# Column and row scans on one core: the order of layer 1's last stages, and how x is brought in

## Chip, cores and metric

The kernel runs on one core of a Trainium2 chip. The metric is the device time of one execution in microseconds, as the median of the runs.

## What is computed

Two layers of the same form. Each normalises x (32 images, 48 channels, 64 rows, 128 columns) over 16 channel groups, runs four scans over the result, and adds the outcome to x. The step of a scan is a convolution with five taps over the other axis, on all 48 channels, plus a bias and the next line of input:

```
def step(w, b):
    def f(carry, inp):
        nxt = inp + _conv1d(carry, w, b)
        return (nxt, nxt)
...
x = x + _L0_conv_ref(_gn(x), ...)      # down, up, right, left
x = x + _L1_conv_ref(_gn(x), ...)
```

Down and up run over the 64 rows (126 steps), right and left over the 128 columns (254 steps). Every step needs the one before it.

## The kernel before

The batch is cut into four groups of eight images. A **row stage** runs down and up for one group, a **column stage** right and left for a pair of groups at once. `PHASES` lists twelve stages, and they run one after the other; I call them r00, r01, c00 and so on: r or c, the layer, then the group or the pair. The profile's tiles carry the same names (`step_00d` is a down step of group 0 in layer 0, with `u`, `r`, `l` for the other ways).

A step (`step`, L824) is nine fp32 products on TensorE into three PSUM tiles; for each tile VectorE then adds bias and input in one operation (L846) and writes the next line. That chain of 2024 steps sets the order of everything else. Around it a list of dated entries, the agenda, holds all other work: `at(t, fn, ...)` puts an entry at step t, and `catch_up` emits the entries that are due before each step. `in_order` keeps each engine's instructions in that order, so what an engine does first is written by hand, and a DMA that waits holds up the later DMAs of its queue. Most DMAs go on SP's queue, some on ScalarE's (ACT), and the loads of a seam partly on POOL's.

**On chip** three slots of 48 KB a partition hold lines. A row stage uses two; a column stage cuts the width into four quarters, keeps three in slots and sends the first to DRAM and back (`spill_unit`). A quarter has six units: three blocks of 128 partitions in each of two groups.

**A row stage** (`plan_rows`, L949) loads its rows 16 at a time from DRAM (`move_rows`, 20 DMAs on SP), normalises them on ScalarE (`scale_rows`, L667) and writes the result of the up scan back. **A column stage** (`plan_cols`, L992) loads quarters, and in the left scan takes each unit through: a residual comes in (`load_residual`), POOL adds it (`add_residual`, L769), and the sum is kept. In layer 0 it goes to DRAM as layer 1's input (`keep_result`), and statistics of it are taken on VectorE (even units) and ScalarE (odd ones). In layer 1 the unit is permuted to the order of the output on POOL and ScalarE (`permute_unit`, L794) and stored (`store_result`), in pieces of 128 bytes. For the first pair, c10, three of the four quarters are instead held in DRAM (`HELD`, `hold_result`, one DMA a unit on ACT's queue) and passed on to the output during c11 (`let_result`, on SP's queue).

Where a column stage follows the row stage of its own second group (`follows`), the last rows go straight from SBUF to the columns' slot (`send_row`, `send_rest`): I call this a **seam**. c00 and c01 have one. c11 follows c10, and c10 follows r13; neither has one.

**The start** (`first_group`, L1126) brings in group 0: sixteen DMAs of 768 KB load one image each, first the upper 16 rows of both halves of the height for all eight images, then the other 16 (I call each of these loads an image). VectorE takes statistics of each as it lands. Rows are then brought to the order of the scan: POOL and ScalarE copy a row's pieces (`permute`, L621), `put_out` stores the row in DRAM, and `move_rows` loads it back with channels and columns spread over partitions. Rows 0 to 3 go through TensorE instead (`rows_by_product`, L1210, with the result copied by ScalarE). The weights of the first scan are laid out by TensorE too (`place_kernel`). At the end stands `scaling` (L341), which averages the statistics on TensorE and turns them into a scale and an offset.

x in DRAM is kept by channel and half of the height, 96 partitions at a time:

```
source = [
    [
        dram.tile([PX, MOIETY], F32, tag=f"xin{g}", name=f"xin{g}")[:, 0 : CHANNEL // 2]
        for g in range(NGRP)
    ],
    kept("mid"),
]
```

Of the kernel before, what the change touches and what calls it, by code (L numbers as in the profile page):

```python
# [78 lines left out]
def weight_runs():  # L79
# [33 lines left out]
    ("rows", 1, 2),  # L113
    ("rows", 1, 3),
    ("cols", 1, 0),
# [5 lines left out]
def kernel(  # L121
# [65 lines left out]
    def kept(name):  # L187
# [6 lines left out]
    MOIETY = (CHANNEL + PAD) // 2  # L194
    source = [
        [
            dram.tile([PX, MOIETY], F32, tag=f"xin{g}", name=f"xin{g}")[:, 0 : CHANNEL // 2]
            for g in range(NGRP)
        ],
        kept("mid"),  # L200
    ]
# [11 lines left out]
    HELD = (2, 1, 0)  # L213
# [13 lines left out]
    def x_by_row(t, e, h0, h1):  # L227

        s, h = divmod(h0, HALF)
        t = t.rearrange("(c s) (i q a e n) -> s e a c i q n", s=2, i=E8, q=NQ, a=NH // 2, e=E8)  # L230
        t = t[s, e, h // E8, :, h % E8 : h % E8 + h1 - h0]
        return t.rearrange("c i q n -> c (i q) n")

    def x_by_col(t, e, j):


        return t.rearrange("(c s) (i q n) -> i q c s n", s=2, i=E8, q=NQ)[e, j]

    def lines(t, h0, h1):

        t = t.rearrange("p (i q a n) -> a p i q n", i=E8, q=NQ, a=NH // 2)[h0 // E8]
        return t[:, h0 % E8 : h0 % E8 + h1 - h0].rearrange("p i q n -> p (i q) n")
# [70 lines left out]
    def load_masks(dma):  # L313
        for s in range(2):
            dma(sided(mask_sb)[s], mask[SIDES[s], SIDES[0]])

# [24 lines left out]
    def scaling(key, layer, g, averages, masks, slack=0):  # L341
# [5 lines left out]
        pool = nc.gpsimd  # L347
# [19 lines left out]
        def small(name):  # L367
# [5 lines left out]
        scale, offset = (  # L373
            stat_pool.tile(
                [FULL, NG, GB], F32, tag=f"{t}{layer}{g}", name=f"{t}{layer}{g}"
            )
            for t in ("scale", "offset")
        )
        coeffs[layer, g] = scale, offset
        mean, var = ps[:, 1 : 1 + NG], ps[:, 2 + NG :]  # L380
        spare = small("dev")
        dev = spare[0 : FULL if n > 1 else PX, 0:n]
        if not slack:
            far = ps[0:PX, 1 + NG : 2 + NG]
            nc.vector.tensor_tensor(far, mean_p, ps[0:PX, 0:1], ALU.subtract)
            nc.vector.tensor_tensor(dev, mean_p, ps[0:PX, 0:1], ALU.subtract)
            nc.vector.tensor_tensor(far, far, dev, ALU.mult)
            nc.vector.tensor_tensor(dev, far, var_p, ALU.add)
            yield
            expand(var, dev[:, 0])  # L390
            yield
            nc.vector.tensor_scalar(var, var, GN_EPS, None, ALU.add)
            r0 = small("std")
            nc.scalar.activation(r0, var, AF.Sqrt)
            expand(mean, mean_p[:, 0])
            yield
            yield
            nc.vector.reciprocal(r0, r0)
            nc.vector.tensor_tensor(var, var, r0, ALU.mult)
            nc.vector.tensor_tensor(var, var, r0, ALU.mult)  # L400
            nc.vector.tensor_scalar(var, var, -0.5, 1.5, ALU.mult, ALU.add)
            nc.vector.tensor_tensor(scale, var, r0, ALU.mult)
            nc.vector.tensor_tensor(offset, mean, scale, ALU.mult)
            nc.vector.tensor_scalar(offset, offset, -1.0, None, ALU.mult)
            return
        mean_s = small("mean")
        if n > 1:
            mean_c = stat_tile([PX, GB], "mean_c", key)
            nc.vector.tensor_copy(mean_c, ps[0:PX, 0])
            yield  # L410
            expand(mean, mean_c)
            yield
            nc.vector.tensor_tensor(dev, mean_p, mean, ALU.subtract)
            nc.vector.tensor_copy(mean_s, mean)
        else:
            nc.vector.tensor_tensor(dev, mean_p, ps[0:PX, 0:1], ALU.subtract)
        pool.tensor_tensor(dev, dev, dev, ALU.mult)
# [5 lines left out]
        if n == 1:  # L423
            expand(var, dev[:, 0])
        else:
# [5 lines left out]
            expand(var, var_c)  # L431
        yield
        var_s = small("var")
        nc.vector.tensor_scalar(var_s, var, GN_EPS, None, ALU.add)
        std = small("std")
        nc.scalar.activation(std, var_s, AF.Sqrt)
        if n == 1:
            expand(mean, mean_p[:, 0])
        yield
        if n == 1:  # L440
            nc.vector.tensor_copy(mean_s, mean)
# [6 lines left out]
        pool.tensor_tensor(t0, var_s, r0, ALU.mult)  # L448
        pool.tensor_tensor(t0, t0, r0, ALU.mult)
        yield  # L450
        pool.tensor_scalar(t0, t0, -0.5, 1.5, ALU.mult, ALU.add)
        pool.tensor_tensor(scale, r0, t0, ALU.mult)
        pool.tensor_tensor(offset, mean_s, scale, ALU.mult)
        pool.tensor_scalar(offset, offset, -1.0, None, ALU.mult)

# [167 lines left out]
    def put_out(g, r, perm):  # L623


        n = perm.shape[-1] // (W * GB)
        dma(lines(source[0][g], r, r + n), perm.rearrange("p (m n) -> p m n", n=LINE))
# [8 lines left out]
    def move_rows(k, h0, h1, to_dram, q=None):  # L636
# [4 lines left out]
        for h in range(h0, h1, E8):  # L641
            end = min(h1, h + E8)
            for o in range(NG):
                for e, c0, c1, p0 in pieces(o):
                    here = view[p0 : p0 + c1 - c0, o, h % HALF : h % HALF + end - h]
                    if to_dram or layer:
                        there = by_row(t, e, h, end, q)[c0:c1]
                    else:
                        there = x_by_row(t, e, h, end)[c0:c1]
# [29 lines left out]

    def scale_first(k, h1, split):  # L680

# [310 lines left out]
    def plan_cols(k, t0, prev):  # L992
# [39 lines left out]
        if layer:  # L1032
            tiles += spare_tiles[0 : 2 if final else 1]
# [303 lines left out]
```

## Time and profile before

| | us |
|---|---|
| median of 3 runs (4236.17, 4236.53, 4246.85) | 4236.53 |
| the profiled execution | 4246.85 |
| its span, first to last instruction | 4245.1 |

What lies around the span is 1.75 us. The stages of that execution, from the first to the last sum that VectorE makes in each:

| stage | from | to | length |
|---|---|---|---|
| start | 0 | 74.09 | 74.09 |
| r00 | 74.09 | 351.10 | 277.01 |
| r01 | 352.01 | 600.05 | 248.04 |
| c00 | 608.37 | 1123.23 | 514.86 |
| r02 | 1124.08 | 1391.78 | 267.70 |
| r10 | 1392.57 | 1643.85 | 251.28 |
| r03 | 1644.64 | 1892.73 | 248.09 |
| c01 | 1900.02 | 2403.76 | 503.74 |
| r11 | 2404.62 | 2667.45 | 262.83 |
| r12 | 2668.24 | 2916.30 | 248.06 |
| r13 | 2917.09 | 3165.15 | 248.06 |
| c10 | 3165.86 | 3661.80 | 495.94 |
| c11 | 3662.66 | 4166.24 | 503.58 |
| tail | 4166.24 | 4245.10 | 78.86 |

How to read it: the shortest row and column stages are those in which no step waited, so the length of another one less that is what its steps waited for, together with the slower steps that follow a wait. In lines of the timeline the columns are start, duration, engine, line, operation, tiles and count; brackets give the idle time before and what ended it. In lines by stage they are the window, its length, then busy time and count of PE, PEld, DVE, ACT and POOL, the granted clock, the share of the 16 DMA engines that was busy, and GB/s.

### The profile page before, as it was taken

Reading aid. Unit: us, or ns where it says so; the run is one execution under the profiler, and the core shown is the slowest. Engines: PE = TensorE matmul, PEld = TensorE weight load, DVE = VectorE, ACT = ScalarE, POOL = GpSimd, SP = SyncE. Lnnn points to the kernel's source line nnn. Section 1 sums busy time; section 2 is a strip of 40 time slices with the busy share of each in tenths; the row PEclk is TensorE's granted clock in tenths of the full one; section 3 lists DMA queues with packets and bytes.
Section 4 is the critical chain, followed back from the end, with each engine's and each line's share of the span. In section 5 each row is a group of like instructions: output and inputs, shape, how many; then the busy total and the mean of one; then the engine's idle time right before and its main releaser. Section 6 shows DMA issues by size and latency. Waiting matters only on the chain. (4 is left out here: it accounts for less than half of the span.)

```text
span 4245.1 us, 90421 instructions
## 1 busy us (share of the span) xinstructions
PE 4072.4 (96%) x36704; PEld 4050.5 (95%) x36704; DVE 2142.6 (50%) x6517; ACT 1346.5 (32%) x2680; POOL 870.8 (21%) x879
## 2 busy tenths in 40 slices
PE   6999999899999999999999999999999999999992
PEld 5899999899999999999999999999999999999992
DVE  6454444457654454444447654444444444444443
ACT  4675001436885446000007863603000012110122
POOL 5460011334423020010014410000000024510352
PEclk9999999999999999999999999999999999999996
DMA  9999668868979999358409979839288049999999
GB/s 229 187 212 155 109 121 178 228 151 261 199 166 181 165 166 152 64 100 182 120 12 274 207 147 155 131 63 162 41 146 188 1 84 251 244 251 159 173 209 182
DMA packets 2129378, 679.80 MB, mean 160 GB/s; under 512 B 2012497, under 2 KB 2062913, under 8 KB 2095169
## 3 DMA queue, kind: packets, MB, share of 16 engines
q1 hardware_dynamic: 2026720, 582.07, 70.7%
q10 hardware_dynamic: 99680, 86.43, 9.5%
q8 instruction: 289, 4.73, 0.5%
q0 software_dynamic: 2560, 5.51, 0.5%
q14 instruction: 129, 1.05, 0.1%
HBM read 397.00 MB, written 295.14 MB: 163 GB/s over the span
## 5 line engine op out<-in xcount | busy, mean ns | idle before, releaser
L667 ACT ACTIVATE arena<-arena,offset,scale 128x256 f32<-128x256 f32 (+2 forms) x816 | 576.6, 800 | 355.0 <-DVE arena L846 122.1
L769 POOL TENSOR_TENSOR arena<-arena 128x2048 f32<-128x2048 f32 x80 | 363.0, 4553 | 1400.7 <-PE step_10l L837 437.5
L621 POOL COPY arena<-arena 96x256 f32<-96x256 f32 x452 | 267.5, 646 | 519.8 <-DMA arena<-in_x 481.0
L564 ACT ACTIVATE early<-arena 128x256 f32<-128x256 f32 x192 | 129.5, 675 | 450.6 <-POOL arena L769 444.5
L837 PE MATMUL step_00r<-arena,early 128*128 128x128 f32 x2286 | 253.6, 275 | 18.9 <-DVE arena L846 11.2
L837 PEld LDWEIGHTS step_00r<-arena,early 128*128 128x128 f32 x2286 | 252.9, 186 | 19.6 <-DVE arena L846 13.3
L837 PE MATMUL step_01r<-arena,early 128*128 128x128 f32 x2286 | 253.2, 274 | 9.6 <-DMA arena<-arena 5.8
L837 PEld LDWEIGHTS step_01r<-arena,early 128*128 128x128 f32 x2286 | 252.4, 186 | 10.3 <-issue 5.3
L837 PE MATMUL step_11r<-arena,early 128*128 128x128 f32 x2286 | 251.1, 273 | 5.2 <-DVE arena L846 5.2
L837 PEld LDWEIGHTS step_11r<-arena,early 128*128 128x128 f32 x2286 | 250.6, 185 | 5.6 <-DVE arena L846 5.6
L837 PE MATMUL step_00l<-arena,wleft 128*128 128x128 f32 x2286 | 249.1, 272 | 0.0
L837 PEld LDWEIGHTS step_00l<-arena,wleft 128*128 128x128 f32 x2286 | 248.6, 184 | 0.0
L837 PE MATMUL step_10l<-arena,wleft 128*128 128x128 f32 x2286 | 248.5, 272 | 0.0
L837 PE MATMUL step_10r<-arena,early 128*128 128x128 f32 x2286 | 248.5, 272 | 0.0
L837 PE MATMUL step_11l<-arena,wleft 128*128 128x128 f32 x2286 | 248.5, 272 | 0.0
L837 PE MATMUL step_01l<-arena,wleft 128*128 128x128 f32 x2286 | 248.4, 272 | 0.0
L837 PEld LDWEIGHTS step_10l<-arena,wleft 128*128 128x128 f32 x2286 | 248.4, 184 | 0.0
L837 PEld LDWEIGHTS step_10r<-arena,early 128*128 128x128 f32 x2286 | 248.4, 184 | 0.0
L837 PEld LDWEIGHTS step_11l<-arena,wleft 128*128 128x128 f32 x2286 | 248.4, 184 | 0.0
L837 PEld LDWEIGHTS step_01l<-arena,wleft 128*128 128x128 f32 x2286 | 248.4, 184 | 0.0
L794 ACT COPY arena<-arena 128x256 f32<-128x256 f32 x172 | 99.4, 655 | 400.9 <-POOL arena L769 136.9
L261 ACT COPY early<-arena 128x1 f32<-128x1 f32 x2 | 0.4, 192 | 657.3 <-DVE arena L846 657.3
(203 smaller groups left out, 7163.7 us busy)
## 6 DMA issues: line engine op xcount, KB each, us to landing
arena<-in_x SPq DMA_DIRECT2D x24, 1536.0 KB, 11.6
xin<-arena SPq DMA_DIRECT2D x48, 768.0 KB, 5.4
arena<-xin SPq DMA_DIRECT2D x96, 384.0 KB, 8.2
mid<-arena SPq DMA_DIRECT2D x96, 384.0 KB, 7.7
arena<-mid SPq DMA_DIRECT2D x192, 192.0 KB, 4.3
upb<-arena SPq DMA_DIRECT2D x192, 192.0 KB, 3.9
arena<-upb SPq DMA_DIRECT2D x96, 384.0 KB, 12.1
arena<-xin SPq DMA_DIRECT2D x186, 192.0 KB, 4.3
```

Source lines behind the costliest of these rows:

```text
L261: fn(*args)
L564: nc.scalar.activation(junk[:, 0:n], view[:, b], AF.Identity, accum_out=self.sum[:, i, j : j + 1])
L621: copy(dst[:, r, q], src[:, r0 + r, q])
L667: nc.scalar.activation(args[0], args[0], AF.Identity, bias=args[2], scale=args[1])
L769: eng.tensor_tensor(unit, unit, nat, ALU.add)
L794: copy(by_w(perm)[:, a], src[:, a])
L837: nc.tensor.matmul(part(whole(ps[o])[0:m], -s), weights[:, i, at : at + m], part(src(i), s), start=seen[o] == 1, stop=seen[o] == left[o],)
```

## The change

In layer 1 the rows of the fourth group (r13) move between the columns of the two pairs: r12, c10, r13, c11. So c11 gets a seam. All four quarters of c10 are held in DRAM; its residuals and the held units go on SP's queue, with four buffers instead of five. They are passed to the output on ACT's queue: the first 30 of 64 items during r13 from step 48, the others during c11 from step 36 to 122. Ahead of each stands a one-element copy on ScalarE that reads the result of a given step (`pace`), so that the item is not issued before that step.

x in DRAM is kept by channel alone, so `put_out` makes two DMAs of 48 partitions where it made one of 96, and the loads of rows and residuals lose their own forms. At the start the first weights come by small DMAs on ACT's queue (taps to DRAM, then 25 pieces to SBUF) instead of through TensorE, the masks and ten bias pieces behind them; rows 4 to 7 come by a second product on TensorE instead of through DRAM; rows 0 to 7 of the first eight loads are copied through DRAM at the very end, for the rows 32 to 39 that they hold besides (before, rows 0 to 3 at the end and 4 to 7 early); and the scale is applied to the first four rows by VectorE alone, row 0 first. `scaling` has one form for all groups. The early activation that loaded ScalarE's table for square roots is gone.

```diff
     ("rows", 1, 2),
+    ("cols", 1, 0),
     ("rows", 1, 3),
-    ("cols", 1, 0),
     ("cols", 1, 1),
...
-    HELD = (2, 1, 0)
+    HELD = (3, 2, 1, 0)
...
     def hold_result(j, i, perm):
         o, half = UNITS[i]
-        dma(held[j, half][o], perm, nc.scalar)
+        dma(held[j, half][o], perm)
...
-                dma(in_output(j, half, e)[c0 * NH : c1 * NH], src[at : at + (c1 - c0) * NH])
+                dst = in_output(j, half, e)[c0 * NH : c1 * NH]
+                dma(dst, src[at : at + (c1 - c0) * NH], nc.scalar)
+
+    def pace(k, n):
+
+        if PHASES[k][0] == "rows":
+            done = row(k, n + 1 if n < H - 1 else 2 * H - 3 - n)[:, 0, 0:1]
+        else:
+            kb, e = divmod(n + 1, E8)
+            j, kk = divmod(kb, KQ)
+            done = quarter(k, j)[:, 0, 0, e * RUN + kk * GB :][:, 0:1]
+        nc.scalar.copy(junk[:, BN - 1 :], done)
...
-        if layer:
-            tiles += spare_tiles[0 : 2 if final else 1]
+        if final:
+            tiles += spare_tiles
...
-                at(end + 63 + 1.9 * n, let_result, *what)
+                if n < 30:
+                    m = 48 + int(2.3 * n)
+                    at(end + m, pace, k + 1, m - 2)
+                    at(end + m, let_result, *what)
+                else:
+                    m = 36 + int(2.6 * (n - 30))
+                    at(end + 2 * (H - 1) + m, pace, k + 2, m - 2)
+                    at(end + 2 * (H - 1) + m, let_result, *what)
...
-            if layer:
-                dma(here, by_col(t, e, j)[c0:c1], nc.scalar)
-            else:
-                dma(here.rearrange("p (s n) -> p s n", s=2), x_by_col(t, e, j)[c0:c1])
+            dma(nat[p0 : p0 + c1 - c0], by_col(t, e, j)[c0:c1], nc.scalar if k == len(PHASES) - 1 else None)
...
+    source = [kept("xin"), kept("mid")]
...
-        dma(lines(source[0][g], r, r + n), perm.rearrange("p (m n) -> p m n", n=LINE))
+        for s in range(2):
+            h = s * HALF + r
+            dma(
+                lines(source[0][g], h, h + n),
+                sided(perm)[s].rearrange("p (m n) -> p m n", n=LINE),
+            )
...
-        pool, act = nc.gpsimd, nc.scalar
-        load_kernel()
         for i in range(2):
             for b in range(GB):
...
+                take_in(0, i * rows, parts[i], slice(b, b + 1))
+        nc.vector.memset(spare["right"], 0.0)
+        nc.vector.memset(spare["left"], 0.0)
+        load_weights("down0", 0, DOWN, aside)
+        load_constants(aside)
         make_ident()
-        place_kernel()
-        spread_masks()
         for b in range(GB):
             stats.take(0, parts[0], b)
-        put_rows(0, 4, 8, free, pool, act)
+        permute_rows(0, 8, 12, free, nc.gpsimd, nc.scalar)
+        put_rows(0, 8, 12, free)
         rows_by_product(0, 4)
-        put_rows(0, 8, 14, free, pool, act)
-        put_rows(0, 14, 16, free, pool)
-        move_rows(0, 4, 8, False)
-        move_rows(0, 8, 16, False)
+        spread_masks()
+        permute_rows(0, 12, 15, free, nc.gpsimd, nc.scalar)
+        put_rows(0, 12, 15, free)
+        permute_rows(0, 15, 16, free, nc.gpsimd)
+        put_rows(0, 15, 16, free)
+        rows_by_product(4, 4)
...
+        move_rows(0, 8, 16, False)
+        for r in range(0, 8, 2):
+            permute_rows(1, r, r + 2, free, nc.gpsimd)
+            put_rows(1, r, r + 2, free)
         for _ in scaling("x0", 0, 0, stats, x_masks):
             pass
-        scale_first(0, 4, 5)
+        scale_at_once(0, 0, 1, nc.vector)
+        scale_at_once(0, 1, 4, nc.vector)
         scale_rows(0, 4, 8)
         scale_rows(0, 8, 16)
-        put_rows(1, 0, 8, free, pool)
         move_rows(0, 16, 24, False)
         scale_rows(0, 16, 24)
...
-        put_rows(0, 0, 4, later, pool)
-        move_rows(0, 32, 40, False)
+        permute_rows(0, 0, 4, later, nc.gpsimd)
+        put_rows(0, 0, 4, later)
+        permute_rows(0, 4, 8, later, nc.gpsimd)
+        put_rows(0, 4, 8, later)
+        move_rows(0, 32, 48, False)
         scale_rows(0, 32, 40)
```

## Prediction

> **What bounds the kernel now.** I read the page first, then the busy time by stage, then the timeline of each engine over the first 75 us and over the starts of the stages.
>
> ```profile
> PE 4072.4 (96%) x36704; PEld 4050.5 (95%) x36704; DVE 2142.6 (50%) x6517; ACT 1346.5 (32%) x2680; POOL 870.8 (21%) x879
> ```
>
> ```profile
> core 0: us, PE busy (x) PEld busy (x) DVE busy (x) ACT busy (x) POOL busy (x), PEclk, DMA share, GB/s
> 0.00:74.09 74.09, 45.26 (x122) 30.02 (x123) 52.55 (x104) 20.97 (x43) 26.71 (x66) 1.00 0.96 246
> 74.09:351.10 277.01, 259.73 (x2277) 257.42 (x2277) 125.75 (x399) 189.37 (x431) 145.33 (x204) 0.97 0.97 194
> 1124.08:1391.78 267.70, 261.10 (x2324) 260.13 (x2323) 139.44 (x443) 185.49 (x367) 79.28 (x106) 0.97 0.91 177
> 1900.02:2403.76 503.74, 499.14 (x4567) 498.76 (x4567) 281.79 (x833) 130.28 (x307) 82.03 (x19) 0.99 0.63 153
> 2404.62:2667.45 262.83, 257.47 (x2324) 256.69 (x2323) 138.92 (x443) 154.64 (x261) 33.32 (x27) 0.99 0.95 159
> 2917.09:3165.15 248.06, 248.06 (x2264) 248.06 (x2263) 120.65 (x378) 3.79 (x6) 0.51 (x1) 1.00 0.60 104
> 3165.86:3661.80 495.94, 495.94 (x4568) 495.94 (x4567) 244.50 (x762) 46.47 (x81) 105.95 (x65) 1.00 0.65 146
> 3662.66:4166.24 503.58, 497.99 (x4561) 497.36 (x4559) 244.39 (x763) 66.64 (x116) 159.59 (x102) 0.99 1.04 201
> 4166.24:4245.10 78.86, 0.00 (x0) 0.00 (x0) 23.69 (x19) 18.92 (x33) 12.73 (x18) 0.51 1.28 173
> ```
>
> TensorE is busy 96%: the kernel is one chain of 2024 steps. Undisturbed, a row stage takes 248.06 us (r13, 126 steps of 1.97) and a column stage 495.94 (c10, 254 of 1.95). No step changes, so the change can only move what stands beside the steps: the start (74.09), waits in stages (r00 loses 277.01 - 248.06 = 29.0; r02, after c00, 19.6; r11, after c01, 14.8; c01 7.8; c11 7.6) and the tail (78.86).
>
> **The start.** Four views give the prices:
>
> ```profile
> 3.09 28.22 SPq L250 DMA_DIRECT2D arena<-in_x  x16
> ```
> ```profile
> 3.38 1.27 ACTq L250 DMA_DIRECT2D mask_in<-in_mask  x2
> ```
> ```profile
> 12.75 0.38 POOL L323 COPY mask_x<-mask_in 96x48 f32<-96x48 f32 x2 [8.66 <-DMA mask_in<-in_mask]
> ```
> ```profile
> 8.80 2.47 DVE L474 BATCH_NORM_STATS2 bn_x<-arena 96x6 f32<-96x512 f32 x4 [5.92 <-DMA arena<-in_x]
> 12.33 2.47 DVE L474 BATCH_NORM_STATS2 bn_x<-arena 96x6 f32<-96x512 f32 x4 [1.06 <-DMA arena<-in_x]
> ...
> 56.57 2.40 DVE L474 BATCH_NORM_STATS2 bn_x<-arena 96x6 f32<-96x512 f32 x4
> ```
> ```profile
> 31.12 16.71 PE L1210 MATMUL rows<-arena,early 96*128 96x512 f32 x18 [7.57 <-DMA arena<-in_x]
> 47.65 2.00 PE L1210 MATMUL rows<-arena,wleft 96*128 96x512 f32 x2
> 59.52 0.46 PE L352 MATMUL ps_x<-mv_x_x,mask_x 96*96 96x8 f32 x2 [9.87 <-DVE mv_x_x L477]
> ```
>
> The first image (issued at 3.09) is used at 8.80, 5.7 us later; the next ones follow every 3.15 us as long as several are in flight, the eighth at 31.0, the last at 56.5. Two 9 KB mask loads, issued on ScalarE's queue from 3.38 to 4.65, are not used before 12.75: a small load comes in just behind the image that was ahead of it (8.80, 12.33).
>
> The changed program puts 42 small DMAs on ScalarE's queue (5 taps, 25 weight pieces, 2 masks, 10 biases) beside the 16 images. In its instruction order SP and ScalarE share a ring of eight DMA semaphores, each DMA waiting for the one eight places before. So image 3 waits for the fifth tap, image 4 for weight piece 6, image 5 for piece 12, image 6 for image 5, image 7 for piece 25, image 8 for a bias. With each small load behind the image ahead of it, images go one at a time: the second lands at about 10, six links of 5.7 + 0.3 to 0.6 (landing, next issue) give the eighth at about 46, and the last eight, issued together, 8 x 3.15 later at 71. That is 14.6 us after today's 56.5. The other end is 0: small loads landing at once.
>
> The Trainium skill (*DMA: Bandwidth & Descriptors*, Queues, rings and completion order) has each DMA engine take turns between queue rows packet by packet. By it a small load would wait for one packet, and if that is a fraction of an image the links and this term would shrink towards 0. The mask rows show a whole image ahead of each small load, and I take 14.6.
>
> Rows 4 to 7 now come by a second product instead of through DRAM. One product is twenty instructions, 18.5 us from 31.12 to 49.65. Two from 46 keep TensorE until 83, and the average that stood at 59.52 queues behind them: +23.5. Its cost was hidden before under the loads. The skill (*TensorE: Matmul & The Clock Gate*, Part 1: The HAM clock gate) releases the array to full rate after about 3.4 us of sustained work; by it the second product could run in half, and the average come near 74. The twenty instructions take 0.9 us each from first to last over 18.5 us, so I keep 18.5.
>
> After the average, today's coefficients take 6.1 us (59.52 to 65.6); one copy moves ahead of the reciprocal, +0.5. The first four rows then took VectorE 6.17 us in fifteen pieces; now row 0 takes two operations on 384 elements and rows 1 to 3 two on 1152. At 2.28 us for 2048 (VectorE's sums in the tail) that is 0.9 and 2.6, and TensorE starts after the first pair. First sum at 83 + 6.6 + 3.5 = 93 instead of 74.09: +19.
>
> Against this stand the later rows of r00. Copies by POOL cost 2.37 us a row (16 in 9.38 us), and three groups of eight rows follow the last image: 57 us, five waits of some 3 us for a buffer's store, then store, ten loads (some 10 us to issue) and ScalarE's scaling (11 us for 8 rows, 46 pieces in 21.0). Rows 32 to 39 are ready at 71 + 57 + 15 + 26 = 169, rows 24 to 31 one group and two waits (25) earlier, at 144. Rows 4 to 15 only wait for ScalarE, 24 pieces at 0.40 and 24 at 0.46 from 89.6: row 8 is ready at 110.2 and wanted at 108. Row 24 is then wanted at 142, row 32 at 162. Each longer wait costs about 2 more, since the steps after it run at half clock (the granted clock reads 0.5 after today's). Losses in r00: 2.4 + 4 + 9, today's 4.5 near step 100 (VectorE's statistics of group 1), 0.3 for the slow first steps: 20.2 instead of 29.0. Start and r00 together: 19 + 20.2 - 29.0 = **+10.3**, between -4.3 (images as today: everything 14.6 earlier) and +20 (five more waits of POOL at 2 us).
>
> Storing x of groups 1 to 3 takes 96 DMAs instead of 48, each 0.3 to 1.2 us to issue on SP. They stand in c00, r02 and r10, beside steps; where SP is late they cost what it is late by (c00 waits 11.55 us at 809.68 for a quarter queued there). **+1**, 0 to 5. The same bytes as residuals of layer 0 in one run rather than two: 0. The coefficients of later groups take one VectorE copy more each, 0.2 us in a step's slack: 0, at most 1 in all.
>
> **Layer 1.** c10 now follows r12 as it followed r13: no loss. r13 comes after columns, as r02 and r11 do (19.6 and 14.8 lost). Of r11's 14.8, 5.8 are VectorE's statistics, which layer 1 hasn't; 9.0 are rows 32 to 63 scaled late (waits for ScalarE's L667 of 1.8 at row 32 and 4.11 at row 48, and slow steps after), behind loads queued on SP and ScalarE's statistics (13.7 us a unit, 2428.66 to 2442.4). Here ScalarE has 2.9 us of permutes a unit instead, but holding a unit on SP's queue waits for those, with the next residual (four buffers instead of five) and r13's row loads behind it: **+5**, from 0 to 20 (r02's). Holding the fourth quarter too is 6 MB more each way in c10, where the DMA share is 0.65 and no step waits: 0, or the 4 us that a late residual would push into r13. c11 now opens with a seam:
>
> ```profile
> 1900.02 0.35 DVE L846 SCALAR_TENSOR_TENSOR arena<-step_01r,bd,arena 128x128 f32<-128x128 f32 x1 [7.29 <-DMA arena<-arena]
> ```
> ```profile
> 3791.94 0.61 DVE L846 SCALAR_TENSOR_TENSOR arena<-step_11r,bd,arena 128x128 f32<-128x128 f32 x2 [5.37 <-DMA arena<-upb]
> ```
>
> At c01 the seam costs 7.29 less a usual 0.8, and 7.8 in the stage: 14.3; at c00, less its late third-quarter wait, 11. **+13**, 10 to 20. The wait at 3791.94, for a quarter behind c10's results, goes with its neighbour: **-7.6**, nothing late next there (c01 has none at that place). Eighty passes to the output leave SP for ScalarE, each behind a 0.2 us copy that waits for a step. Behind them on ScalarE stand only later passes and, after c11's step 122, what it does today. From 3870 to 3935 the passes moved 10.22 MB in 65 us on full DMA engines, so one of 384 KB takes 2.5 us; they now come at one in 3.4 to 3.8: hidden, and in the seam only if late, since the last before it is due at step 114 of 126. The seam's 30 loads on POOL's queue find POOL idle there. The tail stays 78.9: it is DMA at a share of 1.28 on results that are not passed.
>
> Sum: 10.3 + 1 + 5 + 13 - 7.6 = **+21.7**. The profiled execution took 4246.85 (span 4245.1), the highest of three with median 4236.53; I put the sum on the median: 4258.
>
> **Rivals.** A, images not held up: the mask rows came behind images of a full queue, and links with one image may be shorter. Then +21.7 - 14.6 = +7, 4244; it ends within 0.3% once the links save 9 of the 14.6. B, r13 loses what r02 does (+15 more) and the seam, with passes just before, 20 instead of 13: +44, 4280; for it, r02 and r11 had DMA shares of 0.91 and 0.95 and r13 gets passes on top. C, faster: passes no longer crowd c11. DMA share there is 1.04, 1.24 from 4000 on; fourteen items fewer of 4/3 passes at 2.5 us are 47 us of DMA. If the tail is their backlog, 21.7 - 47 gives 4211; it decides from 35 us off the tail. Against it: the last pass lands near 3954 and the share from 3950 to 4000 is 0.77, so the backlog had drained.
>
> **How the numbers follow.** Forecast 0.50, A 0.25, B 0.18, C 0.07. The range takes the forecast, the upper half of A and most of B: 4238 to 4278. What a measurement here can tell is about 0.3%, 12.7 us: slower 0.68 (forecast, B), same 0.25 (A), faster 0.07 (C).
>
> **What would show it.** Right: the last image's statistics near 71, TensorE's products until 83, first sum near 93, a wait near row 32; r13 near 253, c11 with 7 us or more before its first sum and no wait at step 63. Wrong: the last image near 57, or a tail under 60.

## The result, and the profile after

The changed kernel takes 4395.97 us (median of four runs, 4386.05 to 4400.78) against 4239.19 for the kernel before on the same chip: a ratio of 1.0364, 95% interval 1.0340 to 1.0388. I had forecast 4258. The profiled execution took 4393.91 us with a span of 4391.9, 146.8 more than the span before.

The line of the engines on the page of the kernel after:

```profile
PE 4077.6 (93%) x36648; PEld 4044.6 (92%) x36648; DVE 2167.8 (49%) x6503; ACT 1350.8 (31%) x2727; POOL 896.7 (20%) x916
```

TensorE is busy for 4077.6 us where it was for 4072.4, so nearly all of the 146.8 us are waits. Busy time by stage of the kernel after shows where they stand (start, r00, r02, r13, c11, tail):

```profile
core 0: us, PE busy (x) PEld busy (x) DVE busy (x) ACT busy (x) POOL busy (x), PEclk, DMA share, GB/s
0.00:111.63 111.63, 42.87 (x68) 18.56 (x69) 73.62 (x90) 18.26 (x34) 50.63 (x103) 1.00 0.86 205
111.63:401.21 289.58, 257.01 (x2272) 255.14 (x2270) 126.19 (x399) 185.15 (x423) 127.77 (x174) 0.94 0.83 168
1173.28:1433.53 260.25, 257.23 (x2324) 256.77 (x2323) 139.28 (x443) 175.82 (x354) 79.60 (x106) 0.99 0.90 177
3461.09:3739.80 278.71, 253.64 (x2258) 252.57 (x2256) 121.40 (x378) 79.42 (x138) 50.25 (x39) 0.95 1.02 172
3773.51:4304.26 530.75, 503.22 (x4562) 501.98 (x4561) 244.42 (x763) 50.21 (x111) 108.44 (x69) 0.97 0.88 157
4304.26:4391.90 87.64, 0.00 (x0) 0.00 (x0) 26.60 (x19) 18.92 (x33) 22.24 (x22) 0.52 1.28 173
```

| part of the span | forecast, us | measured, us |
|---|---|---|
| start, r00 and r01, to the first sum of c00 | +10.3 | +50.4 |
| c00 to r12 | +1 | -10.9 |
| c10 | 0 | +0.3 |
| r13 with the gap ahead of it | +5 | +38.2 |
| seam and c11 | +13 - 7.6 | +60.0 |
| tail | 0 | +8.8 |
| sum | +21.7 | +146.8 |

**The start.** SP's queue and TensorE in the timeline of the kernel after:

```profile
0.73 41.26 SPq L231 DMA_DIRECT2D arena<-in_x  x16
```
```profile
41.75 16.74 PE L1139 MATMUL rows<-arena,early 96*128 96x512 f32 x18 [41.75 <-DMA arena<-in_x]
...
60.13 16.57 PE L1139 MATMUL rows<-arena,early 96*128 96x512 f32 x18
```

SP needs 41.26 us to issue the sixteen images (28.22 before), 28.0 of them in waits for ScalarE's small loads (8.2 for taps, 11.9 for weight pieces, 7.9 for biases), and two products follow one another, 18.5 us each. VectorE and POOL over the same stretch:

```profile
67.13 2.40 DVE L435 BATCH_NORM_STATS2 bn_x<-arena 96x6 f32<-96x512 f32 x4
...
79.45 0.54 DVE L372 TENSOR_TENSOR dev_x<-dev_x,mv_x_x 96x8 f32<-96x8 f32 x1
...
83.75 22.65 DVE L402 TENSOR_TENSOR dev_x<-var_x,std_x 128x24 f32<-128x24 f32 x1
```
```profile
76.45 13.86 POOL L582 COPY arena<-arena 96x256 f32<-96x256 f32 x24
...
101.72 4.64 POOL L582 COPY early<-arena 96x256 f32<-96x256 f32 x8
108.64 4.56 POOL L582 COPY wleft<-arena 96x256 f32<-96x256 f32 x4 [2.28 <-DMA xin<-wleft]
```

One operation of VectorE on 24 elements lasts 22.65 us, while the five after it last 0.18 each. It ends at 106.40. POOL copies without a gap from 74.15 to 106.36, one copy in 0.573 us. VectorE's operation ends when POOL first pauses. In the kernel before, the same step (L399) and the one operation behind the reciprocal that has all its tensors in SBUF (L404) stood like this, and POOL beside them:

```profile
64.34 0.19 DVE L399 TENSOR_TENSOR ps_x<-ps_x,std_x 128x24 f32<-128x24 f32 x1 [1.20 <-PE ps_x L363]
...
65.45 0.18 DVE L404 TENSOR_SCALAR offset<-offset 128x24 f32<-128x24 f32 x1
```
```profile
63.08 2.37 POOL L621 COPY arena<-arena 96x256 f32<-96x256 f32 x4
67.63 2.40 POOL L621 COPY early<-arena 96x256 f32<-96x256 f32 x4 [2.17 <-issue]
```

**r00.** VectorE's steps in the timeline, and SP's waits from 40 to 215 us (columns: total, times, longest):

```profile
176.01 0.35 DVE L802 SCALAR_TENSOR_TENSOR arena<-step_00d,bd,arena 128x128 f32<-128x128 f32 x1 [14.77 <-ACT arena L630]
...
209.26 0.35 DVE L802 SCALAR_TENSOR_TENSOR arena<-step_00d,bd,arena 128x128 f32<-128x128 f32 x1 [16.19 <-ACT arena L630]
```
```profile
SPq L231 <- ACT arena L630: 44.7, 2, 35.3
```

Rows 24 and 32 come 14.77 and 16.19 us late, scaled by ScalarE. SP had itself waited 44.7 us for ScalarE's scaling of earlier rows before it could store the next ones.

**Layer 1.** VectorE's, then ScalarE's timeline, then SP's waits from 3200 to 3840 us:

```profile
3581.96 0.35 DVE L802 SCALAR_TENSOR_TENSOR arena<-step_13d,bd,arena 128x128 f32<-128x128 f32 x1 [21.44 <-ACT arena L630]
...
3773.51 0.35 DVE L802 SCALAR_TENSOR_TENSOR arena<-step_11r,bd,arena 128x128 f32<-128x128 f32 x1 [33.71 <-DMA arena<-arena]
...
3920.64 0.61 DVE L802 SCALAR_TENSOR_TENSOR arena<-step_11r,bd,arena 128x128 f32<-128x128 f32 x2 [15.99 <-DMA arena<-upb]
```
```profile
3562.88 2.82 ACT L739 COPY arena<-arena 128x256 f32<-128x256 f32 x5 [25.56 <-POOL arena L714]
3565.61 14.12 ACT L630 ACTIVATE arena<-arena,offset,scale 128x256 f32<-128x256 f32 x19
```
```profile
SPq L231 <- DMA out<-held: 70.0, 16, 9.6
```

r13 waits 21.44 us for scaled rows (48 to 63), which ScalarE took up at 3565.61, after standing 25.56 us before a permute that waits for POOL's add. By the trace the last load of these rows had landed at 3550.5, so some 15 of the 21.44 us are this order. The add itself waited for a residual whose last load SP issued at 3550.40, behind the loads of the rows, and which landed at 3558.1. c11 starts 33.71 us after r13 ends, and waits 15.99 at step 63. SP waited 70.0 us in all for passes, which are not on its queue.

### The profile page after: what moved, and what is told of

Same layout as the page of the kernel before. It is cut to its first block, busy times and chain, and to the rows that moved or that the text cites. A ratio compares the mean times of both kernels' runs of the same rounds, so it can differ in the third digit from the quotient of the medians.

```text
span 4391.9 us, 90829 instructions
## 1 busy us (share of the span) xinstructions
PE 4077.6 (93%) x36648; PEld 4044.6 (92%) x36648; DVE 2167.8 (49%) x6503; ACT 1350.8 (31%) x2727; POOL 896.7 (20%) x916
## 3 DMA queue, kind: packets, MB, share of 16 engines
q10 hardware_dynamic: 295520, 71.31, 10.3%
q0 software_dynamic: 3840, 8.26, 0.7%
## 5 line engine op out<-in xcount | busy, mean ns | idle before, releaser
L714 POOL TENSOR_TENSOR arena<-arena 128x2048 f32<-128x2048 f32 x84 | 381.2, 4552 | 1567.3 <-PE step_10l L793 460.8
L793 PE MATMUL step_00r<-arena,early 128*128 128x128 f32 x2286 | 254.3, 275 | 16.6 <-DMA xin<-arena 10.5
L739 ACT COPY arena<-arena 128x256 f32<-128x256 f32 x192 | 110.6, 653 | 396.7 <-POOL arena L714 269.7
L802 DVE SCALAR_TENSOR_TENSOR arena<-step_11r,bd,arena 128x128 f32<-128x128 f32 x381 | 122.3, 348 | 193.5 <-PE step_11r L793 126.1
```

The costliest lines, as they stand in the source:

```text
L714: eng.tensor_tensor(unit, unit, nat, ALU.add)
L739: copy(by_w(perm)[:, a], src[:, a])
L793: nc.tensor.matmul(part(whole(ps[o])[0:m], -s), weights[:, i, at : at + m], part(src(i), s), start=seen[o] == 1, stop=seen[o] == left[o],)
L802: nc.vector.scalar_tensor_tensor(dst(o), whole(ps[o]), bd[:, o, layer, way : way + 1], inp(o), ALU.add, ALU.add,)
```

## The experiments

My theory after this reading had four parts: VectorE shut out by POOL at the start; the halved stores of x ordered behind ScalarE; ScalarE's order of permutes and rows in r13; SP held by the paced passes through the ring of eight semaphores. Each has a rival below. Ratios are to the kernel before on the same chip.

### The start

**a_first**: the mean and the variance of group 0 stay in PSUM (those of groups 1 and 3 too, which share the code), and rows 0 to 3 are scaled as before, fifteen pieces by VectorE and nine by ScalarE. The diffs show only the lines that matter; `...` stands for lines left out between them.

```diff
-        mean = small("mean")
+        mean = ps[:, 1 : 1 + NG] if not slack else small("mean")
...
-        var = small("var")
+        var = ps[:, 2 + NG :] if not slack else small("var")
...
-        scale_at_once(0, 0, 1, nc.vector)
-        scale_at_once(0, 1, 4, nc.vector)
+        scale_first(0, 4, 5)
```

> The changed kernel, with the mean and the variance left in PSUM for the coefficients of group 0, and rows 0 to 3 scaled as before the change (one operation per image and block, by VectorE and ScalarE). Theory: VectorE's product of two operands in SBUF stood still for 22.65 us (83.75 to 106.4) because POOL copied without a pause until 106.36; operands in PSUM and single-tensor operations do not meet POOL. Then the coefficients are ready near 86, the first sum comes near 92 instead of 111.6, and the kernel takes about 4376 (4396 less 20). Rival: VectorE waited for something else, the coefficients stay at 107 and the time at 4396.

Measured: 4390.16 us, ratio 1.0345 (1.0328 to 1.0362). L402 took 0.19 us; the first sum came at 113.86. VectorE's timeline:

```profile
84.69 21.74 DVE L414 TENSOR_SCALAR offset<-offset 128x24 f32<-128x24 f32 x1
```

The wait has moved to the next operation with its operand in SBUF, one with a single tensor, which I had expected to pass.

**a_fused**: a_first with that operation folded into the one before it, which reads PSUM.

```diff
-            pool.tensor_tensor(offset, mean, scale, ALU.mult)
-            pool.tensor_scalar(offset, offset, -1.0, None, ALU.mult)
+            pool.scalar_tensor_tensor(offset, mean, -1.0, scale, ALU.mult, ALU.mult)
```

> As a_first (the coefficients' operands of group 0 in PSUM, rows 0 to 3 scaled as before the change), and the negative of the offset folded into its product, so that no VectorE operation of the coefficients is a lone one-tensor operation on adjoining words of SBUF. In a_first the wait had moved to just that operation: 21.74 us from 84.69 to 106.43, until POOL's copies paused. Theory (VectorE is shut out as long as POOL copies without a gap, by which operations it needs): the first sum comes near 92, r00 keeps its length of about 289, and the time is near 4368. Rival (the wait goes with the moment, whatever the operation): it moves once more, to the scaling of the first rows, and the time stays near 4390.

Measured: 4380.10 us, ratio 1.0337 (1.0318 to 1.0356). The coefficients were done at 84.40, the first sum came at 112.72 all the same. VectorE first waited until 95.57 for a store of x to finish reading; then the first piece of its scaling alone (L657) took 10.69 us, to 106.26, and POOL's run ended at 106.17. So two things held these rows, and removing one shows the other.

**a_layout**: x in DRAM by channel and half, as before; one store of 96 partitions in place of two of every other partition, and the loads of rows and residuals in the form that goes with it.

```diff
-        for s in range(2):
-            h = s * HALF + r
-            dma(
-                lines(source[0][g], h, h + n),
-                sided(perm)[s].rearrange("p (m n) -> p m n", n=LINE),
-            )
+        dma(lines(source[0][g], r, r + n), perm.rearrange("p (m n) -> p m n", n=LINE))
```

> The changed kernel, with x in DRAM kept by channel and half of the height as before the change, so a row's store is one DMA over 96 adjoining partitions instead of two over every other one. Theory: the store that reads every other partition is ordered behind ScalarE's last write to the same tile; that is the 35.3 us for which SP waited before 141.58 and the 9.4 before 177, and it makes the waits of r00 at rows 24 and 32 (14.7 + 1.4 and 15.8 + 2.0). They go: r00 about 256 instead of 289.6, and the time near 4362; if the shorter r02, c01 and r11 of the changed kernel (13 in all) come from its form of x, those go back too and the time is near 4375. Rival: rows 24 and 32 are late since coefficients and ScalarE are late; then r00 stays above 280 and the time above 4385.

Measured: 4355.05 us, ratio 1.0266 (1.0248 to 1.0283). r00 went from 289.58 to 255.99 us; the first sum stayed at 110.42. From 40 to 215 us SP no longer waits for ScalarE's scaling (44.7 us in the changed kernel), and the waits at rows 24 and 32 are gone. So the halved stores stood behind ScalarE's writes; whether the two DMAs or their stride put them there, the runs don't tell.

**a_start**: a_fused and a_layout together, with the 42 small DMAs on POOL's queue.

```diff
-            dma(dst, src, nc.scalar)
+            dma(dst, src, nc.gpsimd)
```

> The changed kernel with three parts of its start mended at once: as a_fused, x by channel and half as in a_layout, and the 42 small DMAs on POOL's queue instead of ScalarE's. Theory: the images no longer wait for small DMAs in the shared ring of eight semaphores, so the last one's statistics come near 57 instead of 67; TensorE's two products end near 68 instead of 78 and the first sum comes near 82 instead of 111.6; r00 takes about 256 and ends near 338 instead of 401. The time is 4333, or 4346 if the later stages lose with the form of x what a_layout's r02 and c01 lost. Rival for the images: they are held up by the small loads on the DMA engines whatever the queue; then the last one stays near 67 and the time near 4345 to 4356.

Measured: 4358.95 us, ratio 1.0289 (1.0268 to 1.0309). The images are back: SP issued them in 28.98 us and the last statistics stood at 56.22 (56.57 before, 67.13 after). But POOL issued small DMAs until 49 us and made the identity matrix for the products only then, so the products ran from 49.47 to 86.1. VectorE's timeline:

```profile
86.69 21.61 DVE L389 TENSOR_TENSOR dev_x<-dev_x 96x8 f32<-96x8 f32 x1
```

Yet another operation, on 8 elements, now takes the wait. The first sum came at 122.58.

**a_port**: a_layout with the whole of before's coefficients for group 0 (PSUM throughout, the last two operations as one) and with rows 0 to 3 scaled by ScalarE, so that of VectorE's work between the average and the first sum only the reciprocal has all its tensors in SBUF.

```diff
+            nc.vector.scalar_tensor_tensor(offset, mean, -1.0, scale, ALU.mult, ALU.mult)
+            return
...
-        scale_at_once(0, 0, 1, nc.vector)
-        scale_at_once(0, 1, 4, nc.vector)
+        scale_rows(0, 0, 4)
```

> The changed kernel with the form of x of a_layout, and nothing left for VectorE in group 0's coefficients and first rows that has both tensors, or its only ones, in SBUF: deviation, mean and variance in PSUM as before the change, the negative folded in, rows 0 to 3 scaled by ScalarE (24 pieces at 0.40). Each of the three runs that mended one such operation had the wait of 21 to 23 us at the next one of that kind. Theory (VectorE is shut out by POOL's unbroken copies whatever it does in SBUF, ScalarE is not): coefficients near 84.5, the first sum near 95 instead of 110.4 in a_layout, r00 256 to 262, the time near 4340. Rival: the start is held by something else at that time; then the first sum stays near 110 and the time near 4355.

Measured: 4348.28 us, ratio 1.0249 (1.0231 to 1.0268). VectorE's timeline, with POOL copying from 74.54 on:

```profile
84.08 0.18 DVE L404 TENSOR_TENSOR scale<-ps_x,std_x 128x24 f32<-128x24 f32 x1
84.30 0.18 DVE L405 SCALAR_TENSOR_TENSOR offset<-ps_x,scale 128x24 f32<-128x24 f32 x1
96.29 0.76 DVE L846 SCALAR_TENSOR_TENSOR arena<-step_00d,bd,arena 128x128 f32<-128x128 f32 x2 [11.82 <-PE step_00d L837]
```

No operation of VectorE was held, and the first sum came 14.1 us earlier than in a_layout. r00 gave 8.4 of it back (264.42 us): ScalarE reached rows 8 and 32 later, and they cost some 7 and 4.7 us where they cost 5 and nothing in a_layout. So the lockout (VectorE's operation standing until POOL pauses) cost some 14 us at the first sum, net of the slower scaling by ScalarE, and about 6 by the end of r00.

### Layer 1

**b_swap**: the kernel before with r13 and c10 exchanged, and four buffers in c10; queues, pieces and start as before.

```diff
+    ("cols", 1, 0),
     ("rows", 1, 3),
-    ("cols", 1, 0),
...
-        if layer:
-            tiles += spare_tiles[0 : 2 if final else 1]
+        if final:
+            tiles += spare_tiles
```

> The kernel before, with only r13 and c10 exchanged, and four buffers instead of five in c10 (the fifth lies over weights that r13 needs). Queues, held quarters, dates of the passes and the start stay as before. Theory: the order itself costs: c10's units that run past its end (some 110 us, under c11 before) now stand in r13 among ScalarE's rows, and c11 opens with a seam behind them; r13 20 to 38 longer with its gap, seam and start of c11 14 to 40, less 7.6: the time between 4270 and 4315. Rival: the order is harmless, and it was the move of held units, residuals and passes to other queues that cost; then r13 near 253, the seam near 13, and the time between 4250 and 4262.

Measured: 4350.45 us, ratio 1.0256 (1.0232 to 1.0280), above the range I expected. The order, with the four buffers that it asks for, costs some 110 us by itself. VectorE's timeline at c11's start:

```profile
3762.53 0.35 DVE L846 SCALAR_TENSOR_TENSOR arena<-step_11r,bd,arena 128x128 f32<-128x128 f32 x1 [54.32 <-DMA arena<-arena]
```

54.32 us ahead of c11 and 24.42 ahead of r13, where the changed kernel has 33.71 and 8.28; r13 itself takes 275.22. On SP's queue stores and passes alternate here, passes taking 8 to 11 us of every 20. The changed kernel's moves between queues shorten the two gaps by 36.8 us and give 34.2 of it back: 25.8 in c11 (504.97 here, 530.75 there), 3.5 in r13 and 4.9 in the tail (82.78 here), which is within what the tail varies by (below).

**a_hold**: c10's residuals and held units back on ScalarE's queue.

```diff
-        dma(held[j, half][o], perm)
+        dma(held[j, half][o], perm, nc.scalar)
```

> The changed kernel, with c10's residuals and held units on ScalarE's queue as before the change. Theory: on SP's queue each held unit waits for ScalarE's permutes, and the next residuals and r13's rows stand behind it; that makes r13's waits at its first step (8.3), at row 16 (4.0) and at row 48 (21.6). Expected: r13 loses about what r11 does, near 258 instead of 278.7, no 8.3 ahead of it, and the time near 4368. Rival: ScalarE itself is late, since it scales rows and permutes units in one order; then r13 stays above 272 and the time above 4388.

Measured: 4387.82 us, ratio 1.0336 (1.0312 to 1.0361). The gap ahead of r13 fell to 3.73, r13 stayed at 278.97: its waits moved to steps 31 and 47. SP's queue alone is not what makes the rows late.

**a_rows**: r13's rows loaded and scaled earlier, so that ScalarE has them ahead of c10's last permutes.

```diff
+            if PHASES[k][1:] == (1, 3):
+                ahead, scaled = (-28, -16, -8, 0), (-13, -2, 6, 14)
```

> The changed kernel, with r13's rows loaded from 28, 16, 8 and 0 steps ahead of its start instead of 28, 12, -4 and -20, and scaled at -13, -2, 6 and 14 instead of -13, 3, 19 and 35. Theory: r13's rows 48 to 63 are scaled at 3565 since ScalarE has c10's permutes ahead of them in its order, and those wait for POOL's adds and these for residuals; c10's units run on until 113 us past its end. With the rows ahead of most permutes r13 takes 260 or less instead of 278.7, and the kernel about 4378. Rival: the rows come late themselves, as their loads wait for the slot that c10's last but one quarter leaves and for SP; then r13 stays above 270 and the time above 4386.

Measured: 4371.97 us, ratio 1.0312 (1.0287 to 1.0337). r13 takes 252.27 us instead of 278.7. So the place of these rows is the cause, on ScalarE behind the permutes for the larger part (15 of the 21.44 us above); the loads were moved along, and no run moves the scaling alone. The gap of the seam grew to 38.97.

**a_pass**: the passes and their pacing copies on POOL's queue, out of the ring.

```diff
-                dma(dst, src[at : at + (c1 - c0) * NH], nc.scalar)
+                dma(dst, src[at : at + (c1 - c0) * NH], nc.gpsimd)
...
-        nc.scalar.copy(junk[:, BN - 1 :], done)
+        nc.gpsimd.tensor_copy(junk[:, BN - 1 :], done)
```

> The changed kernel, with the passes to the output (and the one-element copies that pace them) on POOL's queue instead of ScalarE's. Theory: SP's and ScalarE's DMAs share eight semaphores in turn, so that SP's stores of r13's rows waited 70 us for passes that themselves wait for a step; the seam's sends stood behind them. On a queue with semaphores of its own the same bytes at the same steps hold nobody up: the wait at c11's first step falls from 33.7 to about 8 as in c01, those at its steps 63 and 95 (17.7 and 9.1 with the slow steps) by half or more, and the time to 4340 to 4355. Rival: the passes' bytes, in pieces of 128, keep the DMA engines from the stores; then the wait stays above 25 and the time above 4380.

Measured: 4347.27 us, ratio 1.0241 (1.0210 to 1.0271); the runs spread from 4332 to 4358, and the profile is of the longest. VectorE's timeline at c11's start:

```profile
3771.23 0.35 DVE L802 SCALAR_TENSOR_TENSOR arena<-step_11r,bd,arena 128x128 f32<-128x128 f32 x1 [18.36 <-DMA arena<-arena]
```

The gap fell from 33.71 to 18.36, and c11 from 530.75 to 498.51 us: its waits at steps 63 and 95 are gone. In what is left of the seam, POOL's last passes in r13 stand behind its first loads for the seam, and these loads wait 33.8 us for stores.

**a_fix**: a_port, a_rows and a_pass together, with 20 items in r13 and 44 in c11 instead of 30 and 34.

```diff
-                if n < 30:
+                if n < 20:
...
-                    m = 36 + int(2.6 * (n - 30))
+                    m = 36 + int(2.0 * (n - 20))
```

> All remedies together in the changed kernel: a_port, r13's rows early as in a_rows, and the passes on POOL's queue as in a_pass, with 20 of 64 items in r13 (the last at step 91, ahead of the seam's loads on that queue) and 44 in c11. If the causes add up: a_port's time less 27 (r13) less 48 (seam and c11) less up to 8 for a seam as short as c01's: 4258 to 4275. Rival: they share one cause further back (late SP), so that each alone gives what all give; then above 4300.

Measured: 4270.85 us, ratio 1.0071 (1.0055 to 1.0087). r13 takes 251.07 us, c11 505.36. VectorE's timeline at c11's start:

```profile
3684.93 0.35 DVE L846 SCALAR_TENSOR_TENSOR arena<-step_11r,bd,arena 128x128 f32<-128x128 f32 x1 [7.55 <-DMA arena<-arena]
```

The ratios of a_port, a_rows and a_pass, each less the changed kernel's, sum to -0.0290; together they give -0.0293. So within the intervals the causes add, and these edits take back four fifths of the loss. Of the 28.3 us still left on the span, 8.3 stand ahead of c00, 0.3 in c10, 10.5 in r13 and the gap ahead of it, 8.5 in the seam and c11, and 4.3 in the tail; c00 to r12 take 3.6 off. What makes these is not shown.

### Before, with parts of the change

**b_pass**: the kernel before with its passes on POOL's queue.

```diff
-                dma(in_output(j, half, e)[c0 * NH : c1 * NH], src[at : at + (c1 - c0) * NH])
+                dma(in_output(j, half, e)[c0 * NH : c1 * NH], src[at : at + (c1 - c0) * NH], nc.gpsimd)
```

> The kernel before, with the passes of held units to the output on POOL's queue instead of SP's, at the same steps and without pacing. In the kernel before, c11 waits 5.25 us at its step 63, and about 2.2 in the slower steps after it, for a quarter queued on SP behind passes and results. Theory: with the passes on a queue of their own those 7.4 us go: 4232. Rival: POOL, which adds c10's last residuals until 110 us into c11, falls behind by issuing passes and delays what hangs on it; then 4239 or more.

Measured: 4244.90 us, ratio 1.0010 (0.9999 to 1.0020). c11's wait at step 63 stays (8.55 us, 5.37 before): the passes' place on SP's queue was not what that quarter waited for.

**b_rows**: the kernel before with the rows of r02 and r11 loaded and scaled earlier.

```diff
-            ahead, scaled = (-28, -12, 4, 20), (-13, 3, 19, 35)
+            ahead, scaled = (-28, -12, 2, 6), (-13, 3, 10, 24)
```

> The kernel before, with the lesson of a_rows applied to its two row stages behind columns, r02 and r11: rows 32 to 47 loaded from step 2 and scaled at 10, rows 48 to 63 from 6 and at 24, instead of 4 and 20, 19 and 35, so that they stand ahead of more of ScalarE's statistics. Theory: r02's and r11's waits at rows 32 and 48 (some 7.6 in r02, 9.0 in r11, with the slow steps) go for the most part: 10 to 15 less, 4225 to 4230, faster than both kernels. Rival: the statistics and results that they overtake come later and hold up SP or the coefficients; then 4235 or more.

Measured: 4249.40 us, ratio 1.0020 (1.0009 to 1.0030). In r02 the rows' waits fell to some 2 us, but step 67 now loses 18.9 (some 7 in the kernel before), and r02 takes 273.72 us instead of 267.70. TensorE's timeline in r02:

```profile
1270.33 1.13 PE L352 MATMUL ps_r<-dev_r,mask_r 128*96 128x8 f32 x6 [15.09 <-POOL dev_r L417]
```

The average of group 2's statistics stands among TensorE's steps and waits for a square on POOL, which stands behind copies that wait 28.36 us for their load.

**b_avg**: b_rows with that average begun two steps earlier, ahead of the copies.

```diff
-            t = units[-1][0] + 14
+            t = units[-1][0] + 12
```

> b_rows, with the statistics of a column stage's results begun 2 steps earlier (12 instead of 14 steps after its last unit), so that POOL's square of the deviations stands ahead of its copies of the next 16 rows of group 3, which wait 28.36 us for their load, and not behind them. In b_rows r02 lost nothing at rows 32 and 48 beyond 1.8, but 18.9 at step 67, where TensorE's average waited for that square and the scan behind the average. Theory: that wait goes (it cost 7 in the kernel before, too): r02 near 254 instead of 273.7, the time near 4230, faster than both kernels. Rival: the wait moves to the next step in that chain, or the coefficients of r10 are late; then 4240 or more.

Measured: 4243.95 us, ratio 1.0006 (0.9994 to 1.0017). The wait at step 67 is gone and one at step 84 has come. VectorE's timeline:

```profile
1302.88 0.18 DVE L413 TENSOR_TENSOR dev_r<-mean_r_r,ps_r 128x24 f32<-128x24 f32 x1 [14.07 <-POOL scale L452]
```

The coefficients on POOL are the next to stand behind the copies. No version here beats the kernel before.

## Why the prediction was wrong

The sign held, and the losses stand in the start, r00, r13 and the seam, where I had put them; but the terms for the coefficients, for r00's rows, for r13 and for the seam and c11 were far too small, and in three of them the cause is a wait that I had not seen. By the prediction's own steps:

**Images (14.6).** Right in kind: 10.6. The eighth image came at 41.68 instead of 46. What held the images is the ring of semaphores, not the transfers: SP's waits in the changed kernel name the small loads, and in a_start, on another queue, the same loads leave the images at their old pace. The Trainium skill (*DMA: Bandwidth & Descriptors*, Queues, rings and completion order) has queue rows take turns packet by packet. In a_start the trace fits that, with small loads landing about 1 us apart between images 3.2 us apart. In the changed kernel it does not: the weight piece that ScalarE issued at 9.90 landed at 15.22, beside the image that landed at 15.40, as the mask rows before had it. Why the two queues differ stays open. Rival A asked for 9 of the 14.6 to be saved; 4 were.

**Products (until 83).** They ended at 78.5, having begun at 41.75, 18.5 us each as I had taken them: the second ran no faster than the first, 0.91 us an instruction in both.

**Coefficients ("6.1 us ... one copy moves ahead of the reciprocal, +0.5") and first rows (3.5).** The failed step: 33.3 us instead of 10.1, from the average at 78.34 to the first sum. I priced operations by their durations in the kernel before, where their operands were in PSUM; in the new form both are in SBUF, and POOL was copying. The row operations themselves took 1.1 and 3.0 us for my 0.9 and 2.6. Four kernels show the lockout at four different operations, all with their tensors in SBUF: 21.6 to 22.7 us in three, and 10.69 in a_fused, where it began later. All four ended within 0.1 us of POOL's first pause; no run made POOL pause on purpose. The operations beside it with an operand in PSUM took 0.18 or 0.19, and in a_port, where only the reciprocal (0.30 us, as before) has none, nothing is held. ScalarE was not held in the same way: it waited for the coefficients or a store. The Trainium skill (*SBUF — State Buffer*, Who interferes with whom) says that a VectorE operation with two inputs in SBUF, or a single-input one in a two-port mode, contends with GpSimd (POOL) reading SBUF, that one with at most one input in SBUF and outside those modes does not, and that whoever comes first holds the shared ports for its whole instruction while the other is blocked. The trace agrees on who waits. On how long, it agrees at 79.45 (0.54 us, about one copy) and not at 83.75: one copy would be 0.57, an estimate by that page and the copies' 0.573 us, and it was 22.65, some 39 copies. In the kernel before, L404 fell into a pause of POOL (65.45 to 67.63), and VectorE's scaling, already running when POOL resumed, alternated with POOL's copies from there on (0.58 us a piece instead of 0.25). In a_start the scaling began 0.28 us after POOL had resumed (113.16, 112.88) and alternated all the same, so having begun first is not the condition. Why the two alternate in one case and not in the other stays open.

**Losses in r00 (2.4 + 4 + 9).** Failed at rows 24 and 32: some 16 and 18 us with the slow steps, for my 4 and 9, and 41.5 us in the stage for my 20.2. I had five waits of POOL for a store, but no store that waits for ScalarE. The halved stores did (35.3 + 9.4 us), and with one store of 96 partitions r00 takes 255.99.

**r13 (+5 "as r02 and r11").** Failed: 38.2. I counted ScalarE's 2.9 us of permutes a unit as less than r11's statistics, and passed over when they come: c10's last add starts 113 us after c10's last sum (110 in the kernel before). Before, that tail of work lay beside the columns of c11, which need no scaling. Now each permute waits for POOL's add, and the rows of r13 stand behind it on ScalarE. a_rows puts it back to 252.27; in a_hold, with units and residuals off SP's queue, r13 takes 278.97 all the same. Each long wait also leaves slow steps: the granted clock reads half from 3566.4 to 3586.9, through most of the wait in r13 and some 5 us past it.

**Passes ("hidden, and in the seam only if late") and step 63 ("nothing late next there").** Failed: 60.0 for my 5.4. I used the ring of eight semaphores for the images and not for the passes, which are on ScalarE's queue and so share it with SP. A pass that is paced by a step takes its place in the ring, and SP's later stores wait for it: 70.0 us. The sends of the seam began at 3752.9, 13 us after r13's last sum, where those of c01 began 13 us before r03's. a_pass takes the passes out of the ring and the wait to 18.36, and a_fix leaves 7.55, close to c01's 7.29. There the seam and what c11 loses come to 16 us, so the +13 for a seam was about right once the passes are out of the way. On SP's queue and unpaced (b_swap) the passes cost as much, 54.32 us ahead of c11.

**Rest of layer 0 and the tail.** -10.9 and +8.8 us. In the four kernels with the same code up to there (the changed one, a_hold, a_rows, a_pass) the time from c00's first sum to r12's varied from 2049.0 to 2061.9 us; the kernel before took 2059.9. So the first lies within the spread. The tail varied from 79.5 to 87.7 in six kernels with the same layer 1, and from 77.0 to 81.0 in three with layer 1 as before; I have not settled why, and not all of the 8.8 need be the change's. Rival B had the right places, with 20 us each for r13 and the seam against 38.2 and 60.0. Rival C, a shorter tail, did not come.

## What to carry to other kernels

Reordering stages moves the tail of one stage's side work under another stage: before pricing it, look up when that tail really ends, and list on each engine what will stand behind it. If queues share completion semaphores, every DMA that is paced on purpose can hold up all of them, so give paced transfers a queue outside the ring. A small operation is priced by its duration only where its operands lie in the same memory and the same engines are busy beside it.

## Of the hardware, not expected

- An operation of VectorE on 8 to 24 elements per partition stood for 21.6 to 22.7 us while POOL made 38 or 39 copies of 0.573 us back to back, though two such operations 4 to 5 us earlier, beside the same copies, took 0.49 and 0.54; with an operand in PSUM the same work took 0.18 to 0.19.
- Issuing a pass from POOL's queue takes POOL 1.65 us in the median (a_pass); from ScalarE's queue it takes ScalarE 0.57 (the changed kernel).
